# Multi-query attention block: softmax weights used in the layout of VectorE's block transpose, keys and values by way of DRAM, one-step query chain

## The chip, the cores and the metric

The kernel runs on one core of one Trainium2 chip. The metric is the device time of one execution in microseconds (us). Engines are named PE or TensorE (matmul; PEld is its weight load), DVE or VectorE, ACT or ScalarE, POOL or GpSimd, and SP, whose queue issues most transfers. All data are float32.

## The reference

For each of 64 batches of 128 tokens and 512 features: normalise, make queries for 16 heads of 64, one key and one value shared by all heads, attend with a bias, a causal mask and a key mask and one extra "null" key, project back, normalise, add the input.

```python
xn = layernorm(x, g_in)
q = (xn @ Wq).reshape(b, n, H, DH).transpose(0, 2, 1, 3) * scale
kv = xn @ Wkv
k, v = (kv[..., :DH], kv[..., DH:])
# null_kv (two rows of cond) is put ahead of k and v as one more key and value
sim = jnp.einsum('bhid,bjd->bhij', q, k) + bias
sim = jnp.where(causal_mask, neg, sim)
sim = jnp.where(mask_p[:, None, None, :], sim, neg)
attn = jax.nn.softmax(sim, axis=-1)
out = jnp.einsum('bhij,bjd->bhid', attn, v)
out = out.transpose(0, 2, 1, 3).reshape(b, n, INNER)
return x + layernorm(out @ Wo, g_out)
```

## The kernel before

Batches are worked in groups of four (GB = 4, 16 groups); a group's 512 tokens are normalised (`norm_stats`, `norm_apply`), turned so that features lie on the partitions (`xT`; from group 2 on by VectorE's 32x32 block transpose, `tokens_T`, a write to DRAM, `tokens_out`, and four reads back, `tokens_in`), and multiplied with Wq. Both large products, query and output, are formed with seven block products in place of eight: `token_sum`, `weight_sums` and `out_sums` make the sums of operands, `product` (L436) and `out_product` (L755) the products, numbered 1 to 7, and `keep`, `q_out`, `out_keep`, `out_part` combine them on ScalarE and VectorE. Query products of a group are spread over four steps, one quarter of the features (`f`) a step; output products are made for pairs of batches over two steps, the first of them beginning at batch 1; the last batches (from 59) and batch 0 use a plain product (`out_mm`, L702).

The order on every engine is the order of the calls in the program, which is written out by hand in `step(n)`, n from -6 to 62. A step works on many batches at once: scores of batch n+2, softmax of batch n+1, values of batch n, output of pairs around n-1 to n-3, keys and values of batch n+6, queries of group (n+6)//4, normalisation of batches around n+12.

Causality lets the queries 0 to 63 ("low", half 0) look at keys 0 to 63 alone; queries 64 to 127 ("high", half 1) look at all 128. So `scores` (L500) writes 16 small products of 64 columns, then 16 of 128 columns, each of 64 rows and 64 outputs, a quarter of the array. `scores_add` (L513) adds them to the bias that GpSimd wrote to S[b] (`bias_add`, L479), `scores_max` (L518) takes the row maximum, `exps` (L527) runs 8 exponentials for each half, `rinv` and `scale` (L544, L548) divide.

The softmax weights then lie with queries on the partitions, and the values product needs keys there. `blocks_T` (L580) turns them in blocks of 32 x 32 on VectorE into `sb`; `blocks_move` (L606) moves the blocks, 14 transfers a batch on SP's queue, to the partitions of their keys in `aTb`. `values` and `values_end` (L641) then make 12 products of 64 rows and 64 outputs by 256 columns (where the products are not split, two full-height ones a half take the place of some). `nv` is a copy of the values moved by 64 partitions (`values_move`). The tiny copy `done` (L673) on VectorE orders the high scores behind the first values. The first two batches have their weights turned by TensorE instead (`attn_T_pe`, L615, L620). ScalarE takes the results out of PSUM (L685).

The keys of each batch are written by `kv_out` twice side by side, turned by TensorE (`k_T`, L356) and copied out by VectorE (`kT_out`, L361). The last two products of a query chain, 3 and 4, are issued in the following step (`last`). `product` writes to the PSUM buffers `a`, `c` (pool ps_q, one buffer each) and `w` (pool ps_w, two); output products to `X` and `Y` (ps_y) and `w`; scores to `s` (ps_s, two banks).

SP's queue issues in program order: for each step the block moves, then (`transfers`) the residual input `res`, the next `x`, and where they are due the key mask, the moved values, the stores, and every four steps `xd` and `xT`. From n = B3 = 58 on a special order holds: scores of batch 59 are drawn ahead, a second `aTb` and `sb` are used, part of the moves goes to ScalarE's queue.

Of the kernel before, what the change touches and what calls it, by code (L numbers as in the profile page):

```python
# [8 lines left out]
FP = mybir.dt.float32  # L9
# [8 lines left out]
def kernel(  # L18
# [59 lines left out]
    nc = tc.nc  # L78
# [51 lines left out]
    def loads_late(n):  # L130
        if 1 <= n and not plain(n - 1):
            load_res(n - 1)
        if 0 <= n and plain(n):
            load_res(n)
        for m in (n + 13, n + 14):
            if m < B and (m > 2 * GB + 2) == (m == n + 14):
                load_x(m)
# [100 lines left out]
    aTb = const.tile([P, 6, R8, Q], FP, name="aTb")  # L238

# [9 lines left out]
    xT, qT, kT, vs, nv = {}, {}, {}, {}, {}  # L249
# [80 lines left out]
    ktok = {}  # L330

    def kv_out(m, pkv):
        g, t = divmod(m, GB)
        k = bp.tile([P, 2, DH], FP, tag="ktok", name=f"ktok_{m}")
        nc.vector.tensor_tensor(
            k,
            pkv[:, 0:DH].unsqueeze(1).broadcast_to([P, 2, DH]),
            nkv[:, 0:DH].unsqueeze(1).broadcast_to([P, 2, DH]),
            ALU.subtract,
        )  # L340
        ktok[m] = k
        if t == 0:
            vs[g] = hp.tile([P, GB, DH], FP, tag="vs", name=f"vs_{g}", bufs=3)
        nc.vector.tensor_tensor(vs[g][:, t, :], pkv[:, DH:], nkv[:, DH:], ALU.subtract)

    def values_move(g, ts):

        if ts.start == 0:
            nv[g] = hp.tile([P, GB, DH], FP, tag="nv", name=f"nv_{g}")
        lo, hi = slice(0, DH), slice(DH, P)  # L350
        nc.sync.dma_start(out=nv[g][hi, ts], in_=vs[g][lo, ts])

    def k_T(m, pk=None):
        if pk is None:
            pk = ps_w.tile([P, N], FP, tag="w", name=f"pkT_{m}")
        nc.tensor.transpose(pk, ktok.pop(m).rearrange("p r d -> p (r d)"), ident)  # L356
        return pk

    def kT_out(m, pk):
        kT[m] = hp.tile([P, N], FP, tag="kT", name=f"kT_{m}", bufs=6)  # L360
        nc.vector.tensor_copy(kT[m], pk)  # L361
# [109 lines left out]
    B3 = B - 6  # L471

    def bias_add(b):
        g, t = divmod(b, GB)
        if b in (B3 + 1, B3 + 4):
            S[b] = gp.tile([P, R8, ROW], FP, tag="xT", name=f"s_{b}")
        else:
            S[b] = sp.tile([P, R8, ROW], FP, tag="s", name=f"s_{b}")
        nc.gpsimd.tensor_tensor(  # L479
            S[b],  # L480
            biasp,
            mneg[:, t].unsqueeze(1).broadcast_to([P, R8, ROW]),
            ALU.add,
        )
# [4 lines left out]
    def scores(b, hf):  # L489
# [6 lines left out]
        for f in range(NF):  # L496
            for r in range(2):
                rows = slice(r * DH, (r + 1) * DH)
                for u in range(2):
# [3 lines left out]
                        kT[b][rows, 0:nk],  # L503
# [55 lines left out]
    sb2 = []  # L559
    B2 = B - 8  # L560
    aTbs = [aTb]

    def second_aTb():

        aTb2 = hp.tile([P, 6, R8, Q], FP, tag="xb", name="aTb2", bufs=1)
        nc.gpsimd.memset(aTb2, 0.0)
        aTbs.append(aTb2)

    def aT_of(b):
        return aTbs[b % 2 if b >= B2 else 0]  # L570

    def blocks_T(b):

        if b > B3 and b % 2:
            if not sb2:
                sb2.append(gp.tile([P, 6, R8, Q], FP, tag="qT", name="sb2"))
            sb = sb2[0]
        else:
            sb = hp.tile([P, 6, R8, Q], FP, tag="sb", name=f"sb_{b}", bufs=1)
        nc.vector.transpose(  # L580
            sb.rearrange("p j e q -> p e j q"),
            S[b][:, :, 1 : ROW - 1].rearrange("p e (j k) -> p e j k", k=Q),
        )
        sbs[b] = sb

    def blocks_move(b, take=None):

        sb = sbs[b] if take == 0 else sbs.pop(b)
        count = 0
        for u in range(2):  # L590
            for i in range(2):
                src = slice((2 * u + i) * Q, (2 * u + i + 1) * Q)
                for j in range(3 + i):
                    count += 1
                    if take is not None and count % 2 != take:
                        continue
                    dst = slice(j * Q, (j + 1) * Q)
                    jL = j - 2 * u
                    jU, iU = 2 + j, 2 + 2 * u + i
                    if 0 <= jL <= i:  # L600

                        js, is_ = slice(jL, jU + 1, jU - jL), slice(i, iU + 1, iU - i)
                    else:
                        js, is_ = slice(jU, jU + 1), slice(iU, iU + 1)
                    queue = nc.scalar if take == 1 else nc.sync
                    queue.dma_start(  # L606
                        out=aT_of(b)[dst, is_].rearrange("p s e q -> p s (e q)"),
                        in_=sb[src, js].rearrange("p s e q -> p s (e q)"),
                    )

    def attn_T_pe(b):

        pu = ps_s.tile([P, 2, NF, N], FP, tag="s", name=f"paU_{b}")
        for k in range(R8):
            nc.tensor.transpose(pu[:, k // NF, k % NF, :], S[b][:, k, UK], ident)  # L615
        pl = ps_y.tile([P, R8, DH], FP, tag="X", name=f"paL_{b}")
        for k in range(R8):
            for u in range(2):
                rows = slice(u * DH, (u + 1) * DH)
                nc.tensor.matmul(  # L620
                    pl[rows, k, :],
                    S[b][rows, k, LK],
                    ident[rows, rows],
                    start=True,
                    stop=True,
                )
        for r in range(2):
            nc.vector.tensor_copy(
                aTb[:, 2:, r * NF : (r + 1) * NF, :].rearrange("p s f q -> p f s q"),
                pu[:, r].rearrange("p f (s q) -> p f s q", q=Q),  # L630
            )
        nc.vector.tensor_copy(
            aTb[:, 0:2].rearrange("p s e q -> p e s q"),
            pl.rearrange("p e (s q) -> p e s q", q=Q),
        )

    pos = {}

    def value_mm(b, u, half, keys, vals, slots, start=True):
        for r in range(2):  # L640
            nc.tensor.matmul(  # L641
                pos[b][u][r * DH : (r + 1) * DH, half],
                vals[keys],
                aT_of(b)[keys, slots, r * NF : (r + 1) * NF],
                start=start,
                stop=True,
                skip_group_check=not start,
            )

    lo, hi = slice(0, DH), slice(DH, P)  # L650

    def values(b, split):

        v, moved = vs[b // GB][:, b % GB], nv[b // GB][:, b % GB]
        oT[b] = bp.tile([P, NC, N], FP, tag="oT", name=f"oT_{b}")  # L660
        pos[b] = [
            ps_w.tile([P, 2, 2, NF, Q], FP, tag="w", name=f"po_{b}_{u}")
            for u in range(2)
        ]
        value_mm(b, 0, 0, lo, v, slice(0, 2))
        value_mm(b, 1, 0, hi, moved, slice(0, 2))
        if split:
# [612 lines left out]
```

## Time and profile before

| | us |
|---|---|
| median of 3 runs (lowest, highest) | 1107.68 (1106.34, 1110.6) |
| the profiled execution | 1106.42 |
| its span in the profile | 1104.5 |
| mean granted TensorE clock | 0.997 |

| group of instructions | count | busy us | mean ns |
|---|---|---|---|
| ACT exponentials (L527) | 1024 | 371.5 | 367 |
| POOL bias and mask (L479) | 64 | 205.3 | 3208 |
| POOL scale (L548) | 128 | 189.6 | 1482 |
| DVE scores add (L513) | 128 | 121.6 | 950 |
| DVE max (L518) | 128 | 120.1 | 938 |
| DVE block transpose of weights (L580) | 62 | 109.9 | 1773 |
| PE values (L641) | 1240 records | 115.3 | 379 |
| ACT values out of PSUM (L685) | 128 | 81.0 | 683 |
| PE key transpose, all but three (L356) | 61 | 16.8 | 276 |

How to read it: the records of TensorE overlap, since its matmuls are pipelined; a duration (379 ns) is longer than the distance to the next one, and the distance is what a matmul costs. Each matmul leaves two records. Idle time of an engine that nothing waits for costs nothing.

### The profile page before, as it was taken

To read this page: it belongs to the slowest core of one execution; us is meant where nothing else is said; L and a number is where in the kernel's file an instruction comes from. 1 tells how busy PE (TensorE), PEld (TensorE's weight loads), DVE (VectorE), ACT (ScalarE), POOL (GpSimd) and SP (SyncE) were. 2 spreads that over 40 slices of the span, in tenths; PEclk is the share of its full clock that TensorE was granted. 3 is DMA by queue.
4 is the path that set the end of the run, shared out by engine and by line. 5 is a ranking of instruction groups with operands and counts; after the bars stand their busy time and mean duration, and the time that the engine had idled before them with its cause. 6 is when DMAs were issued, how large, how long until landed. Compare 5 with 4: busy or idle time off the path is not lost.

```text
span 1104.5 us, 27326 instructions
## 1 busy us (share of the span) xinstructions
PE 1081.3 (98%) x9794; PEld 868.1 (79%) x9794; DVE 795.7 (72%) x1729; ACT 665.5 (60%) x2645; POOL 706.0 (64%) x521
## 2 busy tenths in 40 slices
PE   8999999999999999999999999999999999999987
PEld 5576788888888888888888888888888888888643
DVE  4676677877867877776886777787777787666852
ACT  3265567666666656566756566766666665657651
POOL 2546958566676756767575675856667675676832
PEclk9999999999999999999999999999999999999999
DMA  6422354453534444353353435445353453422333
GB/s 198 129 76 62 81 150 112 134 131 89 159 99 139 125 128 122 91 167 107 121 138 113 126 101 149 115 131 132 87 159 99 134 130 116 113 63 76 97 106 100
DMA packets 101062, 129.81 MB, mean 118 GB/s; under 512 B 21312, under 2 KB 65728, under 8 KB 99136
## 3 DMA queue, kind: packets, MB, share of 16 engines
q1 hardware_dynamic: 99680, 126.70, 41.0%
q8 instruction: 78, 1.28, 0.5%
q10 hardware_dynamic: 1248, 1.38, 0.4%
q14 instruction: 56, 0.46, 0.1%
HBM read 54.86 MB, written 31.46 MB: 78 GB/s over the span
## 4 chain that ended last, share of the span: by engine, by line
PE 81%; DVE 5%; DMA 4%; ACT 4%; SPq 3%; POOL 2%; issue 1%; DVEq 0%; POOLq 0%; ACTq 0%
PE pa L436 17%; PE pyX L755 16%; PE pc L436 8%; PE pyY L755 8%; PE ps L500 8%; PE po L641 7%; PE pk L321 4%; PE pw L436 4%; PE pyw L755 4%; DMA x<-in_x_dram 3%; PE py L702 3%; ACT s L527 2%; SPq L606 2%; PE pq L387 1%; DVE s L513 1%
## 5 line engine op out<-in xcount | busy, mean ns | idle before, releaser
L527 ACT ACTIVATE s<-s,nmax 128x65 f32<-128x65 f32 (+1 forms) x1024 | 371.5, 367 | 0.0
L479 POOL TENSOR_TENSOR s<-biasp,mneg 128x1552 f32<-128x1552 f32 x64 | 205.3, 3208 | 112.0 <-DVE sb L580 108.8
L548 POOL TENSOR_TENSOR s<-s,rinv 128x512 f32<-128x512 f32 (+1 forms) x128 | 189.6, 1482 | 122.6 <-DVE nmro L799 89.1
L685 ACT ACTIVATE oT<-po,nv 128x512 f32<-128x512 f32 x128 | 81.0, 683 | 198.0 <-PE po L641 198.0
L527 ACT ACTIVATION_READ_ACCUMULATOR s<-s,nmax 128x1 f32 x1024 | 194.7, 190 | 0.0
L755 PE MATMUL pyX<-wT,oT 128*128 128x256 f32 x696 | 164.7, 379 | 0.5 <-DVE kyu L767 0.5
L755 PEld LDWEIGHTS pyX<-wT,oT 128*128 128x128 f32 x696 | 131.8, 190 | 19.6 <-DVE kyu L767 0.9
L500 PEld LDWEIGHTS ps<-kT,qT 64*64 64x64 f32 x4096 | 92.5, 134 | 48.1 <-DVE s L513 25.6
L513 DVE TENSOR_TENSOR s<-ps,s 128x512 f32<-128x512 f32 (+1 forms) x128 | 121.6, 950 | 10.1 <-PE ps L500 9.6
L436 PE MATMUL pa<-xS,wq 128*128 128x256 f32 x480 | 123.6, 380 | 1.0 <-ACT ku L447 1.0
L518 DVE TENSOR_REDUCE nmax<-s 128x8 f32<-128x520 f32 (+1 forms) x128 | 120.1, 938 | 1.3
L500 PE MATMUL ps<-kT,qT 64*64 64x64 f32 (+1 forms) x4096 | 116.7, 251 | 3.7 <-DVE done L673 2.0
L580 DVE STREAM_TRANSPOSE sb<-s 128x1536 f32<-128x1536 f32 x62 | 109.9, 1773 | 11.6 <-POOL s L548 4.3
L641 PE MATMUL po<-aTb,vs 64*64 64x256 f32 (+1 forms) x1240 | 115.3, 379 | 0.0
L436 PEld LDWEIGHTS pa<-xS,wq 128*128 128x128 f32 x480 | 86.2, 190 | 11.2 <-ACT ku L447 1.8
L447 ACT COPY ku<-pa 128x256 f32<-128x256 f32 x120 | 44.7, 373 | 82.5 <-PE pa L436 82.5
L261 POOL TENSOR_TENSOR rstd<-rstd,nhalf 128x1 f32<-128x1 f32 x64 | 35.7, 558 | 60.4 <-DVE rstd L260 55.4
L436 PE MATMUL pa<-xS,wS 128*128 128x256 f32 x240 | 67.8, 405 | 0.1
L809 ACT ACTIVATE yn<-y,nmro,rstdo 128x512 f32<-128x512 f32 x58 | 45.4, 782 | 36.2 <-DVE nmro L799 36.1
L321 PE MATMUL pk<-wkv,xT 128*128 128x128 f32 x488 | 64.5, 275 | 0.0
L457 DVE TENSOR_TENSOR qT<-pw,kp 128x256 f32<-128x256 f32 x60 | 25.4, 424 | 53.4 <-ACT kp L447 53.4
L641 PEld LDWEIGHTS po<-aTb,vs 64*64 64x64 f32 (+1 forms) x1240 | 55.8, 134 | 9.7 <-issue 4.1
(116 smaller groups left out, 2068.9 us busy)
## 6 DMA issues: line engine op xcount, KB each, us to landing
aTb<-sb SPq DMA_DIRECT2D x369, 64.0 KB
x<-in_x_dram SPq DMA_DIRECT2D x64, 256.0 KB
res<-in_x_dram SPq DMA_DIRECT2D x64, 256.0 KB
out_dram<-y SPq DMA_DIRECT2D x64, 256.0 KB
aTb<-sb SPq DMA_DIRECT2D x492, 32.0 KB
xd<-xb SPq DMA_DIRECT2D x14, 1024.0 KB
xT<-xd SPq DMA_DIRECT2D x56, 256.0 KB
wo<-in_L_cond_Wo_dram SPq DMA_DIRECT2D x1, 2048.0 KB
```

The costliest lines, as they stand in the source:

```text
L321: nc.tensor.matmul(pkv, xT[g][:, t, kc, :], wkv[:, kc, :], start=(kc == 0), stop=(kc == KC - 1),)
L436: nc.tensor.matmul(prod[tag], w[:, kc, f * P : (f + 1) * P], t[:, :, kc, :], start=(start and kc == 0), stop=(kc == HK - 1), skip_group_ch ...
L479: nc.gpsimd.tensor_tensor(S[b], biasp, mneg[:, t].unsqueeze(1).broadcast_to([P, R8, ROW]), ALU.add,)
L500: nc.tensor.matmul(pv[u * DH : (u + 1) * DH, r, f, :], qT[g][rows, f, t, hf, u], kT[b][rows, 0:nk], start=True, stop=True,)
L513: nc.vector.tensor_tensor(sv, pss.pop((b, hf)), sv, ALU.add)
L518: nc.vector.tensor_reduce(nmax[b][:, hf], S[b][:, :, WITH_NULL[hf]], AX.X, ALU.max, negate=True)
L527: nc.scalar.activation(row, row, AF.Exp, bias=nmax[b][:, hf, k : k + 1], accum_out=rsum[b][:, hf, k : k + 1],)
L548: nc.gpsimd.tensor_tensor(sv, sv, rinvs.pop((b, hf)).unsqueeze(2).broadcast_to([P, R8, sv.shape[2]]), ALU.mult,)
L580: nc.vector.transpose(sb.rearrange("p j e q -> p e j q"), S[b][:, :, 1 : ROW - 1].rearrange("p e (j k) -> p e j k", k=Q),)
L641: nc.tensor.matmul(pos[b][u][r * DH : (r + 1) * DH, half], vals[keys], aT_of(b)[keys, slots, r * NF : (r + 1) * NF], start=start, stop=Tru ...
L685: nc.scalar.activation(oT[b][:, u * NF : (u + 1) * NF, :].rearrange("p f (s q) -> p s f q", q=Q), po[u].rearrange("p h i f q -> p (h i) f q"),
L755: nc.tensor.matmul(prod[key], h[:, c, :], w[:, c, :], start=(start and c == 0), stop=(c == HC - 1), skip_group_check=not start,)
```

## The change

The diff has 956 lines; its core follows. `blocks_move`, `aTb`, `attn_T_pe`, `k_T`, `kT_out`, `values_move` and the special order at the end go. The values product takes the weights from `sb` where the block transpose leaves them: strip s of 32 partitions holds, for the keys j, the queries of strip s, so the values are laid out four times, once for each strip (`vr`), and 28 products of 32 rows and 64 outputs are summed over j into four PSUM tiles. Blocks above the diagonal are not formed for even strips (j up to 2), so these have 256 + 128 + 128 columns, odd ones 256 + 256 + 128 + 128.

```diff
-            vs[g] = hp.tile([P, GB, DH], FP, tag="vs", name=f"vs_{g}", bufs=3)
-        nc.vector.tensor_tensor(vs[g][:, t, :], pkv[:, DH:], nkv[:, DH:], ALU.subtract)
...
+    def values_spread(g):
+        vd = dp.tile([P, GB * DH], FP, tag="vd", name=f"vd_{g}")
+        nc.sync.dma_start(out=vd, in_=kvts[g][:, 1].rearrange("p t d -> p (t d)"))
+        vr[g] = hp.tile([P, NQ, GB, DH], FP, tag="vr", name=f"vr_{g}")
+        src = vd.rearrange("(j p) e -> p j e", p=Q)
+        for s in range(NQ):
+            nc.sync.dma_start(
+                out=vr[g][s * Q : (s + 1) * Q].rearrange("p j t d -> p j (t d)"),
+                in_=src,
+            )
+
+    def keys_T(g):
+        kb = hp.tile([P, 2, GB, Q], FP, tag="kb", name=f"kb_{g}", bufs=1)
+        nc.vector.transpose(
+            kb,
+            kvts[g][:, 0].rearrange("p t (c k) -> p c t k", k=Q),
+        )
+        kd = dp.tile([P, 2, GB * Q], FP, tag="kd", name=f"kd_{g}")
+        nc.sync.dma_start(
+            out=kd.rearrange("p c e -> p (c e)"), in_=kb.rearrange("p c t q -> p (c t q)")
+        )
+        kT[g] = hp.tile([P, NQ, GB, Q], FP, tag="kT", name=f"kT_{g}")
+        src = kd.rearrange("(i p) c e -> c p i e", p=Q)
+        for s in range(NQ):
+            nc.sync.dma_start(
+                out=kT[g][s * Q : (s + 1) * Q].rearrange("p i t q -> p i (t q)"),
+                in_=src[s % 2],
+            )
...
+    def values(b):
+        g, t = divmod(b, GB)
+        sb = sbs.pop(b)
+        po = [
+            (ps_w if s % 2 else ps_q).tile(
+                [P, 2, NF, Q], FP, tag="w" if s % 2 else "ac"[s // 2], name=f"po_{b}_{s}"
+            )
+            for s in range(NQ)
+        ]
+        for j in range(NQ):
+            for s in range(NQ):
+                i = s % 2
+                if j > 2 + i:
+                    continue
+                quad = slice(s * Q, (s + 1) * Q)
+                both = j <= i
+                slots = slice(j, j + 3, 2) if both else slice(2 + j, 3 + j)
+                for r in range(2):
+                    rows = slice(r * DH, (r + 1) * DH)
+                    nc.tensor.matmul(
+                        po[s][rows] if both else po[s][rows, 1:2],
+                        vr[g][quad, j, t, :],
+                        sb[quad, slots, r * NF : (r + 1) * NF, :],
+                        start=(j == 0),
+                        stop=True,
+                        skip_group_check=(j > 0),
+                        tile_position=(s * Q, r * DH),
                     )
...
         nc.gpsimd.tensor_tensor(yS[p], h21, h22, ALU.add)
-        nc.gpsimd.tensor_tensor(h21, h11, h21, ALU.subtract)
         nc.gpsimd.tensor_tensor(h11, yS[p], h11, ALU.subtract)
+        nc.gpsimd.tensor_tensor(h21, h22, h11, ALU.subtract)
```

`kv_out` now subtracts the null key and value in one VectorE operation into a tile of the group (`kvts`); `values_out` empties the four tiles with four ScalarE operations of 256 columns. `keys_T(g)` and `values_spread(g)` are called once a group. `pair_residual` is cut in two (`pair_gain`, `pair_residual`). The order is new: the first four steps have a function of their own (`first_step`), then even steps (`step_a`) and odd steps (`step_b`), n from -2 to 63, each ending in `region`:

```diff
+    def region(n, part=None):
+        nb, eb = n + 2, n + 1
+        if nb < B:
+            scores(nb, 0)
+            scores_add(nb, 0)
+        if n >= 0:
+            values(n)
+        if part is not None:
+            out_part(part, 1, "Y", "yu2")
+        if nb < B:
+            scores_max(nb, 0)
+        if n >= 0:
+            values_out(n)
+        if 0 <= eb < B:
+            blocks_T(eb)
+        if nb < B:
+            scores(nb, 1)
+            scores_add(nb, 1)
+            late_max.append(nb)
```

The maximum of the high half is taken in the next step (`max_hi`). In the new even step PE's order is output product 4, kv, query products 1, 2, 6, 5, output 1, query 7, output 2, query 3 and 4; ScalarE's and VectorE's work near its end is

```diff
+        if q:
+            product(g, f, 7, ps_q, "a", start=False)
+            keep("a", "u3")
+            q_out(g, HC + f, hi_t, "c", "u3")
+        if third:
+            pair_norm(p4 + 1)
+        if first:
+            out_product(p12, 2, ps_w, "w")
...
+        if q:
+            product(g, f, 3, ps_q, "c", start=False)
+            q_out(g, f, hi_t, "c", "u2")
+        if soft:
+            exps(e, 1, 3)
+            rinv(e, 1)
+            scale(e, 1)
+        if q:
+            product(g, f, 4, ps_q, "a", start=False)
+            q_out(g, HC + f, lo_t, "a")
+        for m in (n + 12, n + 13):
+            if m < B:
+                load_x(m)
```

In the odd step it is kv (into `Y`), query 1, 2, 6, 5, output 5, query 7, output 6, query 3, output 7, query 4, output 3; the odd step also holds all of the normalisation (two batches), the residual loads, `out_sums`, every fourth step `keys_T`, `values_spread` and `mask_neg`, and, two steps away from these, `tokens_out` and `tokens_in`. The end is

```diff
-    store(B - 3)
-    out_mm(B - 2, 0, NF)
-    values(B - 1, False)
-    values_end(B - 1, False)
-    out_mm(B - 2, NF)
-    out_stats(B - 2)
-    residual(B - 2)
-    store(B - 2)
     out_mm(B - 1)
     out_stats(B - 1)
     store(B - 1)
```

In the changed file `values` is at L591, the copy of query product 4 out of `a` at L459, the reads of keys at L363, values out of PSUM at L607.

## The prediction

> **What bounds the kernel now.** I read the busy shares first, then the chain that ended last, then the busy time of three stretches cut where the work changes, and last TensorE's instructions in order of time.
>
> ```profile
> PE 1081.3 (98%) x9794; PEld 868.1 (79%) x9794; DVE 795.7 (72%) x1729; ACT 665.5 (60%) x2645; POOL 706.0 (64%) x521
> PE 81%; DVE 5%; DMA 4%; ACT 4%; SPq 3%; POOL 2%; issue 1%; DVEq 0%; POOLq 0%; ACTq 0%
> ```
>
> TensorE is the engine that is never free; the others have 28 to 40% of the span to spare. Its row counts an open pipeline as busy, so the places where it loses time are sought in the stretches (us; then busy time and count of PE, PEld, DVE, ACT, POOL; clock; DMA):
>
> ```profile
> 0.00:112.00 112.00, 102.78 (x757) 71.57 (x757) 67.24 (x155) 50.92 (x179) 54.90 (x52) 0.98 0.38 115
> 112.00:997.00 885.00, 883.43 (x8271) 738.16 (x8274) 665.69 (x1458) 559.02 (x2237) 595.38 (x431) 1.00 0.44 121
> 997.00:1104.50 107.50, 95.06 (x775) 58.36 (x773) 62.74 (x116) 55.58 (x231) 55.70 (x39) 0.98 0.35 95
> ```
>
> Stretch two runs from the first product of scores(4) to that of scores(58), 54 steps, with TensorE idle for 1.6 us of 885. There only less TensorE work, or fewer half-hidden waits, can pay. One step of it, PE's order (start us, duration, line):
>
> ```profile
> 588.03 0.69 PE L500 MATMUL ps<-kT,qT 64*64 64x64 f32 x32
> ...
> 603.50 0.69 PE L500 MATMUL ps<-kT,qT 64*64 64x64 f32 x32
> ...
> 620.62 0.69 PE L500 MATMUL ps<-kT,qT 64*64 64x64 f32 x32
> 621.14 0.39 PE L641 MATMUL po<-aTb,vs 64*64 64x256 f32 x2
> ...
> 622.13 1.10 PE L500 MATMUL ps<-kT,qT 64*64 64x128 f32 x32
> 623.05 0.61 PE L641 MATMUL po<-aTb,vs 64*64 64x256 f32 x8
> 623.60 1.13 PE L436 MATMUL pa<-xS,wS 128*128 128x256 f32 x4
> 624.56 0.27 PE L356 MATMUL pk<-ident,ktok 128*128 128x128 f32 x1
> 624.67 1.06 PE L321 MATMUL pk<-wkv,xT 128*128 128x128 f32 x8
> ```
>
> An even step is 15.47 us (588.03 to 603.50), an odd one 17.12. Spacing of starts is the true cost: scores and values together 2.98 us (620.62 to 623.60), the key transpose 0.11, a 128x256 product pair 0.86, so 1.67 ns a column. The page shows two records for each matmul.
>
> **Values, 12 products of a quarter array to 28 of an eighth.** The quarters already run side by side: 16 score products of 128 columns, four a quarter, need 4 x 128 x 1.67 = 0.86 and take 0.92 (622.13 to 623.05). Before, three rounds of 256 columns in each quarter make 3 x 0.43 = 1.28. After, a 32-row strip with odd number has 256+256+128+128 = 768 columns per output half, an even one 512; the longest strip sets 768 x 1.67 = 1.28 again. So the skipped blocks save nothing on the longest strip. No row shows 32-row products. Lower bound: all strips level, 5120 columns over 8 tiles, 1.07. Upper: only two strips at a time, as with 64 rows, 2.56. I take 1.28, nearest to the quarters' 0.92 against 0.86. New is a change of tile size on both sides of the values; its price is here:
>
> ```profile
> 64.19 0.69 PE L500 MATMUL ps<-kT,qT 64*64 64x64 f32 x32
> 64.81 1.13 PE L436 MATMUL pa<-xS,wS 128*128 128x256 f32 x4
> ```
>
> Low scores take 0.62 ahead of another tile size and 0.51 ahead of the same one: 0.10 a change. After: 0.62 + (1.28 + 0.10) + (0.92 + 0.10) = 3.02 against 2.98, +0.04; with the transpose gone (-0.11) a step is some 0.05 shorter, 54 x 0.05 = 2.7 us.
>
> The Trainium skill, "TensorE: Matmul & The Clock Gate", section "Measured speedup vs the span model", speaks against this: four 32-row tiles ran 3.07 times, not 4 times, as fast as one. By that the values would take an estimated 1.67 us, 64 x 0.39 = 25 us more than in my sum, near 1123. The row of the quarters (93% of ideal with four tiles) is why I go without it; no run yet shows 32 rows.
>
> **What hides the rest.** The 861 moves aTb<-sb on SP (some 0.65 us of issue each, 9 to 10 us a step) and `done` go; 10 transfers a group come (kd, 4 kT, vd, 4 vr). Keys are needed a whole step (15 us) after their transpose on VectorE (0.43, from 0.70 for 512 elements and 1.77 for 1536), values three steps later, so both trips through DRAM lie under TensorE. If that cover went, the score product would stand by the trip's length: xd, 1 MB, took 4.3 us to land (75.35 to 79.64), the smaller keys go out and back, so 4 to 8 us a group. VectorE's work falls by 0.5 us a step (0.28 + 0.16 + 0.21 less 0.43 / 4). ScalarE gets four evictions of 256 for two of 512 (1.27 us): 0.37 + 3 x 0.25 = 1.1, no change.
>
> The query chain in one step is the same seven products of 0.86; it frees `a` and `c` for the values. New waits: strip 0 waits for ScalarE's last copy out of `a`, which stands behind five exponentials; strip 2 for DVE's `c`. Walking an even step from its region's start: values leave PSUM 2.2 to 3.4, `max_hi` ends 7.5, rinv 8.3, pair_norm 9.5 to 10.25, residual to 11.65, second pair_norm 12.2 to 12.95, five exponentials of 0.39 to 14.9. Product 4 ends on PE at 15.35, the copy at 15.65, and strip 0 is due at 15.77. Cover: 0.1 us for the copy, 0.45 for the exponentials. Behind the copy wait values_out and the next exponentials; behind strip 0 all of PE. In odd steps product 3 of the output (1.72) comes after product 4, and nothing is near. I take no stall; with the cover gone each us costs 27 us.
>
> **Half-hidden waits.** 27 pairs of 15.40 + 17.13 = 32.53 make 878.3; the stretch took 884.9 (996.9 - 112.0). The 6.6 over lie in one step of four, where x is issued just behind the four 256 KB xT loads and VectorE's statistics wait for it:
>
> ```profile
> 499.13 0.69 DVE L256 BATCH_NORM_STATS2 st<-x 128x6 f32<-128x512 f32 x1 [0.60 <-DMA x<-in_x_dram]
> ```
>
> That step took 17.99. After, both x loads go out at an even step's end behind its second store, and xT a step earlier. Landing took 9.5 us at worst (489.62 to 499.1), and the statistics come 8 us into the next step, so without xT ahead they are in time. I take 5 of the 6.6 as gained (0 to 6.6).
> Stretch two: 884.9 - 2.7 - 5 = 877.2.
>
> **The beginning.** Up to the last plain query products (50.6) nothing moves but three transposes. Then, by PE's order, step -2: kv 0.89 + 7 x 0.86 = 6.9, +1.0 since product 3 follows 7 at once and waits for ScalarE (0.35) and VectorE (0.42), to 58; its region 2.5 without values, to 60.5. Keys of group 0: written 52, out and back 6 (less than twice xd's 4.3), 58; just in time. Step -1, with exponentials, 8.5, region 3.2: 72.2. Step 0: 8.6 and 3.0: 83.8. Step 1: 8 + 7.0 (output of batch 0) + 3.0: 101.8. Step 2: 10.4. Region 2 starts at 112.2, before 112.0; but four query products and a kv more are done by then (4.35 us), and the two weight transposes on PE (2 x 2.1, L615 and L620) are gone. Bounds: 7 us later if keys come behind the 2 MB wo load, 3 earlier if waits overlap.
>
> **The end.** Without query products the softmax of one batch binds: rinv 0.2, scale 1.91, transpose 1.77, scores add 1.21, statistics 1.05 to 1.7, max 1.21, exponentials 3.1 and pair_norms 1.5, some 12 us with wake-ups, against 8 to 11.7 of PE work. From region 56: 16.9 to region 57; then steps 58 to 61 with their regions 16.1 (region 57 in it), 11.9, 12.9, 14.5 (ScalarE's residual stands before the exponentials, GpSimd's bias before the scale); 12.8 to the exponentials of batch 63; 16.4 for the last two outputs and values; 5.6 as before from the last product to the end. Sum 107.1; before 107.6 with 4.35 us more left to do. The special order that goes was worth about that. Bounds 100 to 115.
>
> Sum: 112.2 + 877.2 + 107.1 = 1096.5 of span, against 1104.5. The profiled execution lay 1.9 above its span (1106.42), the median of the runs 1.3 above that. I predict 1098.
>
> **Rivals.** (1) *The 32-row products are slower than quarters.* Each of the four rounds drains before the next: 4 x 0.10 less the one counted, +0.3 x 64 = 19 us, 1117; two strips at a time, +1.28 x 64 = 82, 1180. For: two rounds of unequal length, no such row. Against: the quarters' 93%. It makes the kernel slower from 1.6 us for the values on (15 us over 64 batches). (2) *The copy from `a` comes late:* half a us over its cover in each even step, 27 x 0.5 = 13.5, 1111; for it the thin cover, against it ScalarE's 60%. (3) *Only the steady part gains,* the ends give it back: keys late by 5, the tail at 112: 1108. (4) *The moves are not what costs,* as SP's 861 issues lie off the chain (3%): then x is late still, 1103.
>
> **How the numbers follow.** 0.5% of the median is 5.5 us, about what can be told from no change: faster below 1102.1, slower above 1113.2. Forecast, 1092 to 1102: 0.54. Rivals 2, 3 and 4, 0.22, nearly all within 0.5%. Rival 1, 0.18, and 2 by over a us, 0.06: slower 0.24. The forecast's own range is 1088 to 1104; to hold 8 in 10 it reaches from 1085 (a head or tail at its good end) to 1121, over rival 1's first price.
>
> **What would show it.** After: the L591 products from the start of one strip 0 to high scores in 1.4 to 1.5 us; no idle before them put down to ScalarE's L459 copy; even steps of 15.35, odd of 17.1, none of 18; region 2 near 112, region 56 near 989; idle PE of 15 us or more after 1010. The prediction falls if the values take over 1.6, if even steps are above 15.9, or if keys (L363) hold up scores.

## The result, and the profile after

The changed kernel takes 1127.6 us (median of 4 runs, 1126.6 to 1128.3), the kernel before 1109.1 beside it: a ratio of 1.017, 95% interval 1.014 to 1.019. It is slower, and 29.6 us above the prediction of 1098. The profiled execution has a span of 1126.5 us.

The stretches are cut by TensorE's records: region n starts with the first low score product of batch n + 2.

| us | before | predicted | after | after, order mended (last experiment) |
|---|---|---|---|---|
| start of region 2 | 112.0 | 112.2 | 133.6 | 109.7 |
| region 2 to region 56 | 884.9 | 877.2 | 883.8 | 881.5 |
| region 56 to the end | 107.6 | 107.1 | 109.1 | 101.0 |
| span | 1104.5 | 1096.5 | 1126.5 | 1092.2 |

So 21.4 of the 30 us that separate span and prediction lie in the first ninth, 6.6 in the long middle, 2.0 at the end. The first part of the page of the changed kernel, and its row of the granted clock:

```profile
PE 1085.4 (96%) x11738; PEld 897.4 (80%) x11738; DVE 804.3 (71%) x1554; ACT 694.1 (62%) x2773; POOL 704.1 (62%) x519
PEclk9889999999999999999999999999999999999889
```

TensorE is still what is never free in the middle, but the clock dips in the first slices and in the last. The busy time by stretch (columns as before: us, then busy time of PE, PEld, DVE, ACT, POOL, clock, DMA share, GB/s):

```profile
0.00:112.00 112.00, 92.92 (x582) 63.94 (x583) 65.26 (x121) 43.25 (x144) 46.61 (x45) 0.92 0.39 118
112.00:997.00 885.00, 879.15 (x9912) 755.13 (x9911) 666.12 (x1303) 582.69 (x2341) 594.48 (x431) 1.00 0.33 96
997.00:1126.50 129.50, 113.35 (x1248) 78.30 (x1246) 72.90 (x131) 68.12 (x290) 62.98 (x45) 0.94 0.15 50
```

In the first 112 us TensorE is idle for 19 us (before: 9), and its clock is 0.92 (before: 0.98), while the other engines are no busier there than they were (DVE 65, ACT 43, POOL 47 us of 112). No engine is short of time there, which points to the order of the work. TensorE's records in order of time show the waits; the bracket is the idle time before an instruction and what ended it:

```profile
43.03 2.08 PE L315 MATMUL pkv<-wkv,xT 128*128 128x128 f32 x8 [3.83 <-DVE kvt L330]
44.90 9.20 PE L392 MATMUL pq<-xT,wq 128*128 128x512 f32 x16
...
62.01 1.24 PE L441 MATMUL pa<-xS,wS 128*128 128x256 f32 x4 [3.86 <-POOL xS L423]
63.04 1.91 PE L441 MATMUL pc<-xS,wS 128*128 128x256 f32 x4
...
123.39 1.12 PE L441 MATMUL pa<-xS,wS 128*128 128x256 f32 x4 [4.07 <-ACT kp L452]
124.32 1.89 PE L441 MATMUL pc<-xS,wS 128*128 128x256 f32 x4
```

Three waits of about 4 us, each ended by another engine (VectorE, GpSimd, ScalarE), and behind each, products that last nearly twice as long as elsewhere (1.91 and 1.89 where 1.03 is usual, 9.20 where 7.03 is). Four waits of 0.9 to 2.0 us before query product 3, in steps -2 to 1, come on top. In the middle, one region of the changed kernel:

```profile
591.99 0.69 PE L500 MATMUL ps<-kT,qT 64*64 64x64 f32 x32
592.61 1.56 PE L591 MATMUL po<-sb,vr 32*64 32x256 f32 x56
594.10 1.10 PE L500 MATMUL ps<-kT,qT 64*64 64x128 f32 x32
```

From the start of strip 0 to the high scores: 1.49 us. Odd steps are 17.19, even ones 15.46 and 15.65 in turn; no step of 18 is left.

What stands before the first wait is in VectorE's and GpSimd's queues, here from the timeline of the changed kernel, first VectorE's, then GpSimd's:

```profile
33.30 4.08 DVE L404 TENSOR_TENSOR wS<-wq 128x1024 f32<-128x1024 f32 x1
37.42 4.10 DVE L405 TENSOR_TENSOR wS<-wS,wq 128x1024 f32<-128x1024 f32 x1
41.55 1.22 DVE L406 TENSOR_TENSOR wS<-wq,wS 128x1024 f32<-128x1024 f32 x1
```

```profile
33.11 7.32 POOL L479 TENSOR_TENSOR s<-biasp,mneg 128x1552 f32<-128x1552 f32 x2
```

Before the change the same three sums took 1.21, 1.23 and 1.23 us, with GpSimd's two bias additions behind one more power of a normalisation, from 39.2 on (VectorE's timeline, then GpSimd's):

```profile
33.91 1.21 DVE L399 TENSOR_TENSOR wS<-wq 128x1024 f32<-128x1024 f32 x1
35.16 1.23 DVE L400 TENSOR_TENSOR wS<-wS,wq 128x1024 f32<-128x1024 f32 x1
36.41 1.23 DVE L401 TENSOR_TENSOR wS<-wq,wS 128x1024 f32<-128x1024 f32 x1
```

```profile
39.24 6.37 POOL L479 TENSOR_TENSOR s<-biasp,mneg 128x1552 f32<-128x1552 f32 x2
```

Now the additions start 0.2 us ahead of the first sum. That sum ends 1.1 us after the first bias addition is over (33.11 + 3.2 + 1.1 = 37.4), so it seems to have stood still until then; the third, with GpSimd done at 40.4, takes 1.22. The keys and values of three batches are taken out of PSUM behind the sums, and TensorE waits for that.

### The profile page after: what moved, and what is told of

Its sections match the earlier page's. It is cut to its first block, busy times and chain, and to the rows that moved or that the text cites. A ratio compares the mean times of both kernels' runs of the same rounds, so it can differ in the third digit from the quotient of the medians.

```text
span 1126.5 us, 29916 instructions
## 1 busy us (share of the span) xinstructions
PE 1085.4 (96%) x11738; PEld 897.4 (80%) x11738; DVE 804.3 (71%) x1554; ACT 694.1 (62%) x2773; POOL 704.1 (62%) x519
## 5 line engine op out<-in xcount | busy, mean ns | idle before, releaser
L607 ACT ACTIVATE oT<-po,nv 128x256 f32<-128x256 f32 x256 | 100.2, 474 | 138.2 <-PE po L591 138.2
L563 DVE STREAM_TRANSPOSE sb<-s 128x1536 f32<-128x1536 f32 x64 | 113.4, 1772 | 8.6 <-POOL s L548 3.9
L441 PEld LDWEIGHTS pa<-xS,wq 128*128 128x128 f32 x480 | 92.3, 192 | 14.0 <-POOL xS L423 0.7
L591 PE MATMUL po<-sb,vr 32*64 32x128 f32 (+1 forms) x3584 | 100.3, 323 | 2.4 <-DVE y L697 2.4
L591 PEld LDWEIGHTS po<-sb,vr 32*64 32x64 f32 x3584 | 79.5, 131 | 13.4 <-DVE y L697 2.8
L462 DVE TENSOR_TENSOR qT<-pc,ku 128x256 f32<-128x256 f32 x120 | 49.5, 413 | 40.5 <-ACT ku L452 35.7
L315 PE MATMUL pkv<-wkv,xT 128*128 128x128 f32 x512 | 71.7, 284 | 3.8 <-DVE kvt L330 3.8
L315 PEld LDWEIGHTS pkv<-wkv,xT 128*128 128x128 f32 x512 | 65.0, 193 | 11.0 <-issue 5.3
L441 PE MATMUL pa<-xS,wS 128*128 128x256 f32 x240 | 61.9, 380 | 7.9 <-ACT kp L452 4.1
L441 PE MATMUL pc<-xT,wS 128*128 128x256 f32 x240 | 62.5, 383 | 5.9 <-DVE qT L462 5.9
```

What stands on the lines that cost most here:

```text
L315: nc.tensor.matmul(pkv, xT[g][:, t, kc, :], wkv[:, kc, :], start=(kc == 0), stop=(kc == KC - 1),)
L441: nc.tensor.matmul(prod[tag], w[:, kc, f * P : (f + 1) * P], t[:, :, kc, :], start=(start and kc == 0), stop=(kc == HK - 1), skip_group_ch ...
L563: nc.vector.transpose(sb.rearrange("p j e q -> p e j q"), S[b][:, :, 1 : ROW - 1].rearrange("p e (j k) -> p e j k", k=Q),)
L591: nc.tensor.matmul(po[s][rows] if both else po[s][rows, 1:2], vr[g][quad, j, t, :], sb[quad, slots, r * NF : (r + 1) * NF, :], start=(j == 0),
L607: nc.scalar.activation(oT[b][:, u * NF : (u + 1) * NF, :].rearrange("p f (h i q) -> p i h f q", h=2, i=2)[:, i], po, AF.Identity, bias=nv2,)
```

## The experiments

All start from the changed kernel unless said otherwise. "Start" is the start of region 2 (133.6). In the runs whose program is the same up to there, VectorE's first weight sum begins anywhere from 31.9 to 33.5 us (33.3 in the profile above); a difference in the start of under 2 us in a single run says little.

**Later bias.**

```diff
-        if n == -4:
+        if n == -3:
             bias_add(0)
             bias_add(1)
```

> The changed kernel, with GpSimd's first two bias additions issued one step later (n = -3 in place of -4), so that they no longer run beside VectorE's three weight sums. Theory (GpSimd's new place slows VectorE, the keys and values come out of PSUM late, TensorE waits 3.83 us at 43.0 and then loses its clock): the weight sums take 1.2 us each again, the wait at 43 falls to about 1.5 or less, the next query product takes 7.0 in place of 9.2, and region 2 starts 5 to 7 us earlier than 133.6. Rival (the weight sums are slow for another reason, say the weights' transfers): sums stay at 4 us and nothing moves. Second rival (the bias is then late for scores(0)): the gain is given back before region 2.

Measured: 1121.2 us, start 126.4, 7.2 earlier. VectorE's sums in its timeline:

```profile
33.59 1.22 DVE L404 TENSOR_TENSOR wS<-wq 128x1024 f32<-128x1024 f32 x1
34.84 1.22 DVE L405 TENSOR_TENSOR wS<-wS,wq 128x1024 f32<-128x1024 f32 x1
36.10 1.22 DVE L406 TENSOR_TENSOR wS<-wq,wS 128x1024 f32<-128x1024 f32 x1
```

The wait at 43 is gone and the query product behind it takes 7.03. The sums begin no earlier than in the changed kernel (33.6 against 33.3), so the 7.2 us come from GpSimd's place. The Trainium skill, "SBUF — State Buffer", section "Who interferes with whom", has a rule for it: a VectorE instruction with two inputs in SBUF and a GpSimd instruction that reads SBUF need one and the same read interface, and whichever comes second stands still until the first is through. The 4.08 beside and the 1.22 alone agree with it.

**Token sums ahead of the normalisation.**

```diff
         if n == -3:
             keys_T(0)
             values_spread(0)
+            weight_sum_3()
+            for k in range(1, 3):
+                token_sum(1, k)
             tokens(8)
```

> The changed kernel, with the third weight sum and the two token sums of group 1 issued ahead of the normalisation of batches 8 and 9 (whose two powers stand before them on GpSimd's queue). Theory: product 6 of step -2 no longer waits 3.86 us at 62.0, the two products behind it take 1.03 in place of 1.9, region 2 starts 4 to 6 us earlier than 133.6. Rival (the token sums wait for xT's last copies or for VectorE's third weight sum anyway): the wait shrinks by less than 1.5 us and the start moves by less than 2.

Measured: 1128.6 us, start 134.2: no gain, the theory failed as it stood. The token sums were ready at 58.9, yet product 6 waited just as long, for another engine (TensorE's timeline of this run):

```profile
62.58 1.60 PE L441 MATMUL pa<-xS,wS 128*128 128x256 f32 x4 [4.25 <-ACT kp L452]
```

ScalarE's copy kp stands behind the two `norm_apply` of batches 8 and 9, which wait for the same statistics. The profile of the changed kernel had put the wait down to GpSimd (sums done at 61.95), as the last to come; kp lay only 1.2 us below it (done at 60.77), and the third weight sum, now in front of the statistics on VectorE with its 1.47 us, brought it up. The two in the changed kernel's timeline:

```profile
60.42 0.35 ACT L452 COPY kp<-pa 128x256 f32<-128x256 f32 x1
60.69 1.26 POOL L423 TENSOR_TENSOR xS<-xT,xS 128x512 f32<-128x512 f32 x1
```

By these traces it is the normalisation as a whole that is late, and not the sums alone.

**Later residual.**

```diff
+        if n == 2:
+            residual(0)
+            store(0)
         region(n, n - 2 if second else None)
...
-            residual(n - 1)
-            store(n - 1)
+            if n > 1:
+                residual(n - 1)
+                store(n - 1)
```

> The changed kernel, with the residual and the store of batch 0 issued behind step 2's work in place of step 1's end, so that ScalarE's first exponentials of batch 3 don't stand behind an operation that waits for the output statistics. Theory: the 4.07 us wait of product 6 at 123.4 falls under 1 us, product and output pair behind it regain 0.9 and 0.9 us, region 2 starts 4 to 6 us earlier than 133.6. Rival (the exponentials are late because the high maximum is late): the wait stays above 2.5 us.

Measured: 1127.0 us, start 131.9, of which 1.2 was there already at region -2. Step 2 fell from 20.3 only to 19.8. ScalarE was in time, product 6 had no wait, but product 7 waited 4.09 for GpSimd's third token sum. GpSimd's timeline of this run:

```profile
118.43 0.55 POOL L743 TENSOR_TENSOR rstdo<-rstdo,nhalf 128x1 f32<-128x1 f32 x1 [7.05 <-DVE rstdo L742]
118.95 2.35 POOL L647 TENSOR_TENSOR wT<-wo,wT 128x1024 f32<-128x1024 f32 x1
121.26 3.18 POOL L479 TENSOR_TENSOR s<-biasp,mneg 128x1552 f32<-128x1552 f32 x1
124.41 1.25 POOL L423 TENSOR_TENSOR xS<-xT 128x512 f32<-128x512 f32 x1
```

GpSimd idles 7 us for the statistics of output 0, and a weight sum of the output and a bias come before the token sum. Twice, then, the wait under the named one was as long as the named one.

**Idle products in the three long waits.** They shorten nothing; they only keep TensorE at work.

```diff
         for k in {-4: range(3), -3: range(3, 4)}.get(n, ()):
+            if k == 2:
+                keep_busy(14)
             kv_out(k, kv_mm(k))
...
+            if n in (-2, 2):
+                keep_busy(14)
             product(g, f, 6, ps_q, "a", start=False)
```

> The changed kernel, with 14 idle products of the identity (0.22 us each in the first microseconds of the trace, 3.1 us together) put into each of its three long waits of the beginning (3.83, 3.86 and 4.07 us). They use a score buffer that nothing else needs then, and shorten no wait. Theory (a long wait costs twice, the second time as granted clock): the products behind the waits run at full speed (9.2 back to 7.0 us, 1.9 to 1.03, 1.89 and 2.75 to 1.1 and 1.9), region 2 starts 5 to 8 us earlier than 133.6, with the same work before it. Rival (the products behind the waits are long because of late operands): nothing moves, or the start is later by what the idle products take.

Measured: 1122.7 us, start 128.3. Windows of the changed kernel, and of this one (the clock is the third number from the end):

```profile
40.00:50.00 10.00, 6.97 (x15) 3.98 (x16) 4.57 (x9) 0.00 (x0) 0.98 (x2) 0.66 0.76 252
62.00:70.00 8.00, 7.08 (x52) 5.23 (x52) 2.41 (x5) 1.12 (x3) 3.39 (x2) 0.79 0.40 102
```

```profile
40.00:50.00 10.00, 9.23 (x38) 5.16 (x37) 3.43 (x9) 1.35 (x3) 0.55 (x1) 1.00 0.66 218
62.00:70.00 8.00, 7.08 (x92) 6.00 (x93) 3.72 (x8) 2.79 (x14) 0.00 (x0) 1.00 0.23 70
```

The clock is back at 1.00, the plain query product takes 7.03, the pairs 1.03. From the end of the first long wait to region -2 it took 22.1 us (41.9 to 64.0) in place of 26.4 (43.0 to 69.4): 4.3 us were clock. In step 2 nothing was gained (20.33 against 20.30): with the clock kept, the token sum that the experiment before found became the wait, 2.02 us. The Trainium skill, "TensorE: Matmul & The Clock Gate", section "What's actually happening", says that TensorE's clock is halved after an idle window of about 3.4 us, counted in windows that run freely. The products of 1.91 against 1.03 behind waits of 3.8 us agree.

**Four values products more, four fewer.** The first gives the even strips their fourth round, whose weights are zero; the second leaves it out of the odd strips too.

```diff
-                if j > 2 + i:
-                    continue
```

```diff
-                if j > 2 + i:
+                if j > 2:
```

> The changed kernel, with four more values products a batch: the even strips get their fourth round (keys 96 to 127, weights zero there), so that all strips have 768 columns per output half; 32 products in place of 28, 6144 columns a half in place of 5120. Theory (the longest strip sets the time, 1.28 of the 1.49 us): the values still take 1.47 to 1.52 us from their first start to the high scores, the steps keep 15.46 and 17.19. Rival (a price for each product, 1.49 / 28 = 0.053 us): 1.70, each step longer by 0.21, the span by 13.

> The changed kernel without the fourth round of the odd strips: the keys 96 to 127 are left out of the values of the queries that see them. 24 products, the longest strip has 640 columns. Theory (longest strip): 1.49 - 128 x 1.67 ns = 1.28 us, steps shorter by 0.21, the span by 13. Rival (rounds that drain, or issue that sets the time whatever the length): less than 0.15 off; a price for each product gives 1.28 as well, so this run has to be read beside that with four more.

Measured: 1127.5 and 1116.7 us. TensorE's records of one region, with four more, then with four fewer (line numbers are each kernel's own):

```profile
592.47 1.61 PE L589 MATMUL po<-sb,vr 32*64 32x256 f32 x64
594.01 1.10 PE L500 MATMUL ps<-kT,qT 64*64 64x128 f32 x32
```

```profile
603.01 1.34 PE L591 MATMUL po<-sb,vr 32*64 32x256 f32 x48
604.28 1.10 PE L500 MATMUL ps<-kT,qT 64*64 64x128 f32 x32
```

1.54 with four more, 1.27 with four fewer, against 1.49. A price for each product (0.053) would have made it 1.70; the longest strip sets the time, as the prediction had it, and a product that lengthens no strip costs 0.013, so the four that are skipped save 0.05 us together. Over 768 and 640 columns (1.28 and 1.07) there is a nearly fixed excess, 0.21 and 0.20, where the prediction had 0.10. Steps followed (odd ones 17.24 and 16.97, even ones 15.52 and 15.24), save the even ones of 15.65, which stayed at 15.65 in both: those had another bound.

**The beginning in order.** Too long to show whole: bias(0) and bias(1) behind the weight sums, batches 8 and 9 normalised ahead of the last plain query product, and

```diff
-            if f == 0:
+            if f == 0 and n != 2:
                 token_sum(g, 3)
...
-            for k in range(1, 3):
+            for k in range(1, 5 if n == 1 else 3):
                 token_sum(g + 1, k)
...
-        if 0 <= n < 4:
-            out_weight_sum(n)
+        k = {-1: 0, 0: 1, 2: 2, 3: 3}.get(n)
+        if k is not None:
+            out_weight_sum(k)
```

with residual(0) in step 2, the keys and values of steps -1 and 0 and output 0 between query products 7 and 3, and the statistics of steps -1 and 1 behind the sum that product 3 waits for.

> The changed kernel with the beginning's queues put in order: bias(0) and bias(1) on GpSimd behind the weight sums; the normalisation of batches 8 and 9 a step part earlier, ahead of the last plain query product, so that neither GpSimd's token sums nor ScalarE's copy p1 stand behind it; the third and fourth token sum of group 2, the residual of batch 0 and two weight sums of the output out of step 2's way; keys and values of batches 5 and 6 and output 0 issued between query products 7 and 3; the statistics of steps -1 and 1 behind the sum that product 3 waits for. Theory (queue order in the beginning costs all of the 21.4 us that I missed): waits of 3.8, 3.9 and 4.1 us go, those of 2.0, 0.97 and 2.0 before product 3 shrink under 0.3, clock 1.00 in all stretches, region 2 starts at 110 to 114, span 1102 to 1107. Rival (some of it is work: keys through DRAM, four more query products): region 2 not before 118.

Measured: 1109.9 us, span 1108.1, start 115.3: 18.3 earlier (1.3 of it ahead of any move, as the weight sums begin at 32.0), and short of the 110 to 114 expected. The waits of 3.8 and 4.1 are gone, of the 3.9 there are 1.7 left, those before product 3 are 0.9, 0.4 and twice nothing; but new ones of 3.65 (VectorE's low sum of scores(1), behind the normalisation I had moved) and 2.38 (the same in step 1, behind VectorE's mask) came in.

**Beginning and end in order.** The same, and for the last steps:

```diff
         max_hi()
+        if late_out:
+            out_stats(late_out[0])
...
         (step_b if n % 2 else step_a)(n)
+        if late_out:
+            residual(late_out[0])
+            store(late_out.pop())
```

> The same, and in the last steps (60 to 62) the output statistics behind the high maximum, the residual behind the exponentials; in step 58 the sum of output products 1 and 2 ahead of the gain of the pair before. Theory (the end's 4.4 us wait at 1091 is ScalarE's residual standing before the exponentials and GpSimd's bias behind it, the 2.4 us one at 1047 VectorE's order): both fall under 1 us, from region 56 to the end 100 to 104 in place of 109.1. Rival (the softmax of one batch alone binds these steps, whatever the order): above 107.

Measured: 1110.2 us, span 1108.5. From region 56 to the end 105.6, 3.5 shorter, less than expected; the wait of 4.4 fell to 2.1, since GpSimd's last bias now stood behind the output statistics, and the one of 2.4 to 0.8, with a new one of 1.8 behind it. Its beginning, the same program as the run before, was 3.8 longer, which the last section comes back to.

**More moves.** Batches 10 and 11 behind step -1's region, output 0 in two parts, bias(0) behind the token sums, the last bias and the last exponentials earlier.

> The kernel with head and end in order, and five more moves: batches 10 and 11 are normalised and turned behind step -1's region (their place held VectorE's sum of scores(1) and TensorE 3.65 us); output 0 is cut, two chunks between query products 7 and 3, six between 3 and 4, so that they cover VectorE's slow mask (3.3 us) again; bias(0) behind GpSimd's token sums; in step 61 the last bias ahead of the output statistics; from step 58 the last exponentials ahead of the second pair's normalisation. Theory (what was lost in the beginning is queue order and, behind waits, clock): region 2 starts at 109 to 112 with the clock at 1.00 from 28 us on; region 56 to the end 101 to 104; stretch two stays 883.8; span 1095 to 1099, faster than the kernel before by about 1%. Rival (the beginning has 3 to 5 us that no order takes away, keys through DRAM among them): region 2 not before 114, span above 1101, no difference from before that 5 rounds tell.

Measured (6 runs): 1103.0 us, 0.995 (0.993 to 0.997) of the kernel before. The end is 101.1, as expected; the start is 116.3, as the rival had it. One long wait remained (TensorE's timeline):

```profile
76.49 2.08 PE L441 MATMUL pa<-xS,wS 128*128 128x256 f32 x4 [5.07 <-ACT kp L452]
78.36 1.91 PE L441 MATMUL pc<-xS,wS 128*128 128x256 f32 x4
```

ScalarE waited 5.4 us for a 0.3 us operation of VectorE that I had moved behind the region, with all exponentials and the copy behind it.

**Odd strips first.**

```diff
-            for s in range(NQ):
+            for s in (1, 3, 0, 2):
```

> The same, with the odd strips' values products issued ahead of the even strips' in each round. Theory (the longest strip sets the time and starts late by the issue of the products before it, about 0.014 us each by the run with four more): the odd strips start 0.03 to 0.06 us earlier, values 1.43 to 1.46 in place of 1.49, span 2 to 4 us shorter. Rival (the excess over 1.28 is a fixed price of the change of tile size): 1.49 as before, no difference.

Measured (7 runs): 1104.0 us, no difference from the run before; the values take 1.50. The excess is not the long strips' later start. Whether it is all the price of the change of tile size stays open.

**Normalisation back, transposes behind.** Only `tokens_T` of batches 10 and 11 stays behind the region.

> The kernel with head and end in order (even strips first, as in the changed kernel), with the normalisation of batches 10 and 11 on ScalarE and VectorE ahead of step -1's region again, and only their block transposes behind it. Theory (its place behind the region held ScalarE's exponentials and the copy p1 behind VectorE's queue: one wait of 5.07 us at 76.5, and products of 1.91 in place of 1.03 behind it): the wait falls under 1 us, all products from 28 to 112 us run at full clock, region 2 starts at 108 to 111 in place of 116.3, span 1093 to 1096, 1.2% faster than the kernel before. Rival (a wait of the same size comes up in the next queue): region 2 not before 114, span above 1099.

Measured (6 runs): 1099.1 us, 0.991 (0.989 to 0.992) of the kernel before. The 5 us wait went, step -1 to 0 is 12.0 us, yet the start is at 114.7, where the rival had it: step 1 again had a wait, 2.15 us, which VectorE's mask held.

**The mask ahead of GpSimd's scale.**

```diff
+        if q and f == 3:
+            mask_neg(g)
         if soft:
             rinv(e, 1)
             scale(e, 1)
...
-                if g < NG:
-                    mask_neg(g)
```

> The kernel before this one (order of head and end mended), with VectorE's mask of the next group one place earlier in each fourth step, ahead of the reciprocal that releases GpSimd's scale, so that the two no longer run beside each other. Theory (the mask, 0.6 us when GpSimd is still and 3.0 beside its scale, ends late, the low sum of the scores after it too, and the high scores wait 0.19 us in each second even step, 2.15 us in step 1): the mask takes 0.6 us, all even steps 15.46 in place of 15.46 and 15.66 in turn (13 x 0.19 = 2.5 us), the wait of step 1 at 101 goes (2 us, and 1 of clock): region 2 at 111 to 112, span 1093 to 1095. Rival (the steps of 15.66 have another cause, such as the token sums that follow the scale): they stay, and only step 1 gains.

Measured (4 runs, 1092.9 to 1093.9): 1093.4 us, 0.986 (0.984 to 0.988) of the kernel before. The mask's two operations in the changed kernel (from its timeline), and all operations that touch the mask here (count, shortest, median and longest in ns):

```profile
640.50 2.97 DVE L470 TENSOR_SCALAR mneg<-m 128x256 f32<-128x256 uint8 x2
```

```profile
L470 DVE TENSOR_SCALAR mneg<-m x32: 277/353/421, 29.7 to 1004.7; 128x256 f32<-128x256 uint8 x16, 128x512 f32<-128x512 uint8 x16
```

Beside the scale (640.01 to 641.91 on GpSimd, and token sums from 641.87) one operation takes 1.5 us, ahead of it 0.35. The even steps between region 2 and region 56 are all 15.46 now, and stretch two is 881.5, 2.3 less than the changed kernel's; that one has 12 steps of 15.65, 0.19 over, which makes the 2.3 (the expectation counted 13). The start is 5.0 us earlier than in the run before, more than the 3 us or so expected, but 1.2 of that is there at region -2 already, ahead of the moved mask. Its busy time by stretch:

```profile
0.00:112.00 112.00, 103.35 (x854) 74.33 (x858) 67.00 (x140) 53.91 (x189) 58.06 (x53) 1.00 0.42 126
112.00:997.00 885.00, 885.00 (x9984) 762.19 (x9977) 647.67 (x1318) 587.68 (x2357) 592.91 (x431) 1.00 0.33 97
997.00:1092.20 95.20, 84.30 (x909) 54.40 (x908) 55.05 (x97) 53.12 (x230) 51.07 (x37) 0.95 0.18 57
```

The clock of the first stretch is 1.00, and TensorE is idle for 8.7 us there in place of 19.

## Why the prediction was wrong

**The beginning** is where it fell, in the sentence "Up to the last plain query products (50.6) nothing moves but three transposes". On TensorE that was so. On GpSimd two bias additions moved up beside VectorE's weight sums, on VectorE, GpSimd and ScalarE a normalisation moved down in front of the token sums and the copy p1, and in step 2 the output statistics of batch 0 came to stand before GpSimd's and ScalarE's work. I had walked TensorE's queue and taken every operand as ready. Step by step, as starts of low scores in regions -2 to 2:

| | -2 | -1 | 0 | 1 | 2 |
|---|---|---|---|---|---|
| predicted | 58.0 | 69.0 | 80.8 | 98.8 | 112.2 |
| after | 69.4 | 82.6 | 93.9 | 113.3 | 133.6 |
| last experiment | 56.3 | 66.7 | 78.7 | 95.9 | 109.7 |

Of the 21.4 us, 11.4 are lost up to region -2 (the bias 7.2 of them, by the experiment that moved it; 4.3 of the 11.4 are clock behind waits, a term that the prediction lacked altogether and that overlaps with the 7.2), 3.1 in the next three steps (2.0 of them query product 3, for which I had allowed 1.0 a step: in the odd steps the normalisation's statistics stood before its sum and made it 2.0; the rest is not taken apart) and 6.9 in step 2. The last row shows that TensorE's own work was priced about right: with the queues in another order its four steps take 53.4 us (56.3 to 109.7), where I wrote 54.2. That it also starts 1.7 earlier is no merit of the walk: its weight sums begin at 32.1, those of the profile that I walked from at 33.9. The walk's first sum also has a slip: 50.6 + 6.9 + 1.0 is 58.5 and not 58. The bounds that I gave, keys behind the 2 MB load, named the wrong danger: no score product waited for keys. Nor did any of the three signs come that were to bring the prediction down (values 1.49, even steps of the middle at most 15.67, no score held up by keys); none of them looked at the queues of the beginning.

**The values.** The mechanism was right (strips side by side, the longest one sets the time, skipped blocks save next to nothing), the size off: 1.28 + 0.10 predicted, 1.28 + 0.21 measured, 0.11 x 54 = 5.9 us in stretch two. Rival 1, rounds that each drain for 0.10, would have lost 0.31 with the fourth round; the run with four products fewer lost 0.22, the columns alone. The estimate by the skill's factor of 3.07, 1.67 us, was 0.18 above the measured 1.49.

**The extras of 18 us** went, all 6.6 us of them, where I had counted 5. The rest of stretch two follows: a pair of steps is 17.19 + 15.55 = 32.74 against the 32.43 predicted; 0.22 of the 0.31 are the values, 0.09 the mask beside GpSimd's scale, of which the prediction said that VectorE's load falls and did not ask what runs beside it. Together: 877.2 + 5.9 + 2.3 - 1.6 = 883.8. With the values at their measured size the sign of a term turns, too: without the late x a pair took 32.53 before the change and takes 17.19 + 15.46 = 32.65 after it, even with the mask moved. So the new layout makes TensorE's steady work 0.12 a pair longer, not shorter; what stretch two gains by the last experiment, 3.4 us, is the 6.6 of the late x less 27 x 0.12.

**Rival 3** (the ends give the gain back) was nearest in kind, with keys and the tail as its causes and 10 us as its size, where the queues took 23. **Rival 2** (ScalarE's copy out of `a` late) did not come: strip 0 never waited for it, though the cover was 0.1 us by the walk. **Rival 4** had x late still, and it is not: no step of 18 is left. But its core, that the moves are not what costs, stays open: the change took the moves away and also issued x and xT elsewhere, and no run has the one without the other. **The end** took 109.1 against 107.1; its walk named the two culprits (residual before the exponentials, bias before the scale) and priced them too low; the run that put them in order, with one more sum, gained 3.5 us. That the last experiment's span of 1092.2 lies near the 1096.5 predicted is partly luck: its beginning is 2.5 shorter than the sum has it, its middle 4.3 longer and its end 6.1 shorter. How much of its gain over the kernel before the same care with the order would have brought without the new layout, no run shows.

## What to carry to other kernels

When a change gives a new order, walk the queue of every engine from its start and not the bottleneck's alone: for each operand of the bottleneck, ask what stands before its producer and what that waits for. Where a wait goes, look for the next one under it before counting the gain; here the second was as long in step -2 and in step 2. Where TensorE waits for VectorE, look at what GpSimd runs beside it: here a sum and a mask took three to four times as long beside GpSimd's work. Price a wait of some 4 us on TensorE with the first products behind it at half speed; here two such waits cost 4.3 us on top of their length.

## What the runs showed of the hardware

VectorE's 128 x 1024 sum took 4.08 us beside a GpSimd addition that had begun 0.2 us earlier, and 1.22 alone; its mask 1.5 us an operation beside GpSimd's scale and token sums, 0.35 ahead of them. TensorE's clock depends on more than a wait's length: two runs with the same program up to there, with the same wait of 2.38 us in step 1, went on at different speeds. TensorE's timeline, first of the run with the beginning in order, then of the one with beginning and end in order:

```profile
103.64 1.10 PE L500 MATMUL ps<-kT,qT 64*64 64x128 f32 x32 [2.38 <-DVE s L513]
```

```profile
105.87 1.87 PE L500 MATMUL ps<-kT,qT 64*64 64x128 f32 x32 [2.38 <-DVE s L513]
```

From 104 to 110 us the granted clock is 1.00 in the first and 0.72 in the second. The second lost 1.6 us in that step to the clock (17.8 against 16.2), and 1.3 more behind the 3.65 wait of step -1 (15.7 against 14.4). So a wait of 2.4 us can cost the clock, and the same program can come out some 3 us apart by it. The skill's 3.4 us does not tell these two by their length; windows that run freely could, which no run here shows.
